# Moving the layer norms' statistics within a round of a shifted-window attention block

## The chip, the cores and the metric

The kernel runs on one core of one Trainium2 chip. The metric is the device time of one execution in microseconds (us); lower is better. A core has five engines that run side by side, each through its own list of instructions in order: TensorE (PE in the profile; its weight loads are shown as PEld), VectorE (DVE), ScalarE (ACT), GpSimd (POOL) and SyncE (SP), which here issues nearly all DMA transfers. Engines wait for each other by semaphores. TensorE writes its products to PSUM, from which VectorE and ScalarE take them into SBUF, the working memory.

## The reference

The input x is (16, 192, 56, 56) in fp32. Layer 0 is a Swin block with windows of 7x7 tokens, shifted by 3, 6 heads of 32; layer 1 a depthwise 3x3 convolution whose filters are computed from the image's mean. All biases are 0 and all gains 1 in the inputs, but the kernel uses them.

```python
h = _ln(jnp.transpose(x, (0, 2, 3, 1)), norm1_g, norm1_b)        # first norm, over 192 channels
h = jnp.roll(h, (-SHIFT, -SHIFT), axis=(1, 2))
win = h.reshape(B, nwh, WS, nww, WS, C).transpose(0, 1, 3, 2, 4, 5).reshape(-1, N, C)
qkv = (win @ qkv_w + qkv_b).reshape(-1, N, 3, HEADS, HD).transpose(2, 0, 3, 1, 4)
q, k, v = (qkv[0] * SCALE, qkv[1], qkv[2])
attn = jnp.einsum('bhqd,bhkd->bhqk', q, k) + bias[None]
attn = jax.nn.softmax(attn + mask, axis=-1)
out = jnp.einsum('bhqk,bhkd->bhqd', attn, v).transpose(0, 2, 1, 3).reshape(-1, N, C)
h = out @ proj_w + proj_b
x1 = x + back_to_the_image(h)
y = _ln(jnp.transpose(x1, (0, 2, 3, 1)), norm2_g, norm2_b)       # second norm
y = jax.nn.gelu(y @ fc1_w + fc1_b, approximate=False) @ fc2_w + fc2_b
x = x1 + jnp.transpose(y, (0, 3, 1, 2))
# layer 1, per image
t = relu(bn(x.mean(axis=(2, 3)) @ w1.T))
wt = (t @ w2.T + b2).reshape(b * DIM, 1, 3, 3) * MASK            # 4 taps of 9 are left
out = depthwise_conv(x, wt) + bias
```

## The kernel before

**Strips and rounds.** An image is cut into 8 bands of 7 rows; a strip is two such bands, one in each half of the 128 partitions, with the 192 channels as 3 groups of 64. An image has NU = 4 strips, the input S = 64. x is kept in SBUF for three images at a time (`xt`, slot b % 3); each strip is normed, attended to and passed through the two layers in place. The main loop at the end runs rounds r = -2 to S + 2 and works in each of them on several strips at different stages: scores and values of strip r, weighted values and projection of strip r - 1, first layer of the MLP for strip r - 2, its second layer for strip r - 3, queries and keys of strip r + 1. When an image's last strip has passed the second layer (the round in which `weighing` is true), its filter taps are computed (`taps`, L958 and L970 to L988); its convolution (`conv`, L1137 and L1152) and the stores of its output (L1035) follow in the three rounds after that.

**The order.** Nothing is issued while the loop runs. Each step is recorded by `add(engine, cost, function, reads, writes, lag)` in a `Plan`. Steps of TensorE keep the order in which they are recorded. For all other engines `Plan.order` plays the list through with the given costs and with `lag` as an extra delay after a transfer, and lets each engine take the step that can start first, then the one whose due time is earliest. So the costs and lags set the order, and a step may be issued far from where it stands in the loop. In the built program every engine's order is fixed.

**PSUM.** Four tiles `ps` are handed out in turn by `bank()`. A product that takes a tile waits until the engine that read the tile's last content, four products before, is done with it.

**A norm's statistics.** `statistics(n, s)` squares the strip's rows on ScalarE (`sq`, L299) and adds the three channel groups of x and of the squares on GpSimd into `fold[:, n]` (L306, L308); n = 0 is the first norm, n = 1 the second. `deviations(norms)` multiplies the folds by a block matrix on TensorE (L322), which gives mean and mean square; then Square on ScalarE (L336), a subtraction on VectorE (L343), and Ln and Exp on ScalarE (L352, L359) make 1/deviation in `rs`. SP sends `rs` to a small DRAM tile (`rsd`, L369) and reads it back twice with a broadcast over 64 partitions into `rb` (L378). `scaled1` (L436, L447) multiplies the first norm's rows by it into `xs1`, read by `queries_keys` (L478) and `values` (L673); `scaled2` (L463) does so for the second norm into `xs2`, read by `first_layer` (L838). The means are folded into the weights. The first rounds (`early`, r < 3) use `full_deviations`, which needs no transfer.

**Attention.** `scores` (L558) writes three tiles; VectorE adds the bias (L584) and takes the maxima (L595), GpSimd subtracts them (L600), ScalarE takes the exponential (L607), VectorE the sums (L612, L613), GpSimd divides (L618). `turn_shares` turns the shares in blocks on VectorE (L629) into `tt`, and ten transfers bring them into `pt` (L635). `values` (L673) are copied by ScalarE (L689), moved by eight transfers into `vb` (L699) and turned on VectorE (L708). `weighted` (L728) multiplies both a round later; its three tiles, j = 0 to 2, are copied in four parts each, i = 0 to 3, into `o1` and `o2` (L755 on ScalarE, L757 on VectorE). `projection` (L799, L785) adds onto x on VectorE (L827). The second layer is L876 with its end on VectorE (L863). The first layer's Gelu (L850) needs another table than Ln and Exp; each change is a table load on ScalarE (L1169).

**TensorE's order in a round before the change:** scores, values, weighted, second layer, projection, queries and keys, first layer, and then the product of `deviations` for the first norm of strip r + 2 and the second norm of strip r - 1. `statistics(0, r + 2)` stand at the start of the round, `load(r + 3)` at its end.

Of the kernel before, what the change touches and what calls it, by code (L numbers as in the profile page):

```python
# [40 lines left out]
def flat(keys):  # L41
    return [x for k in keys for x in (k if isinstance(k, Keys) else (k,))]


class Plan:
# [7 lines left out]
    def add(self, eng, dur, fn, reads=(), writes=(), lag=0.0, slack=60.0, by=None):  # L53
        i = len(self.ops)
        deps = set()
        reads, writes = flat(reads), flat(writes)
        for k in reads:
            if k in self.writer:
                deps.add(self.writer[k])
        for k in writes:  # L60
            if k in self.writer:
                deps.add(self.writer[k])
            deps.update(self.readers.get(k, ()))
        for k in reads:
            self.readers.setdefault(k, []).append(i)
        for k in writes:
            self.writer[k] = i
            self.readers[k] = []
        deps.discard(i)
        self.ops.append((eng, dur, fn, sorted(deps), lag, slack, by))  # L70
# [70 lines left out]
def tile_swin_then_dynamic_conv(  # L141
# [29 lines left out]
    S = B * NU  # L171
# [12 lines left out]
    add = plan.add  # L184
# [21 lines left out]
    rb = sb("rb", 128, 2, UT)  # L206
# [18 lines left out]
    rs = sb("rs", 128, HT)  # L225
# [47 lines left out]
    def load(s, by=None, lag=8.0):  # L273
        b, u = divmod(s, NU)
        t = xt[b % 3]
        xv = x[b].rearrange("(g p) r c -> p g r c", p=64)
        parts = [(0, 0, WS, SHIFT + WS * u)]
        first = SHIFT + LR + WS * u
        if u < NU - 1:
            parts.append((1, 0, WS, first))  # L280
        else:
            parts += [(1, 0, IMG - first, first), (1, IMG - first, WS, 0)]
        for h, lo, hi, at in parts:
            def go(h=h, lo=lo, hi=hi, at=at):
                nc.sync.dma_start(
                    t[P(h), :, 1 + WS * u + lo : 1 + WS * u + hi, :],
                    xv[:, :, at : at + hi - lo, :],
                )
            add("SP", 0.2 * (hi - lo), go, writes=[("x", b % 3, u, h) if lo == 0 else ("x", b % 3, u, 2)], lag=lag, by=by)
# [22 lines left out]
    def deviations(norms):  # L312

        p, pk = bank()
        lanes = slice(64 * norms[0], 64 * norms[-1] + 64)

        def product():
            for k in range(2):
                for n in norms:
                    for h in range(2):  # L320
                        c = 64 * n + 32 * h
                        nc.tensor.matmul(  # L322
                            p[c : c + 32, k, 0:HT],
                            blk,
                            fold[:, n, k, h * HT : (h + 1) * HT],
                            start=True,
                            stop=True,
                            tile_position=(0, c),
                        )

        keys = [("f", n, k) for n in norms for k in range(2)]
        add("PE", 0.33 * len(norms), product, keys + ["blk"], [pk])
        add(
            "ACT",
            0.4,
            lambda: nc.scalar.activation(m2[lanes], p[lanes, 0, 0:HT], AF.Square),  # L336
            [pk],
            ["m2"],
        )
        add(  # L340
            "DVE",
            0.36,
            lambda: nc.vector.tensor_tensor(  # L343
                m2[lanes], p[lanes, 1, 0:HT], m2[lanes], ALU.subtract
            ),
            [pk, "m2"],
            ["m2", "variance"],
        )
        add(
            "ACT",  # L350
            0.45,
            lambda: nc.scalar.activation(m2[lanes], m2[lanes], AF.Ln, bias=eps_t[lanes]),  # L352
            ["m2", "eps", "table"],
            ["m2"],
        )
        add(
            "ACT",
            0.4,
            lambda: nc.scalar.activation(rs[lanes], m2[lanes], AF.Exp, scale=-0.5),  # L359
            ["m2", "table"],  # L360
            ["rs"],
        )
        far[0] += 1
        d = rsd[far[0] % 2]
        dk = ("rsd", far[0] % 2)

        def away():
            lo, hi = 4 * norms[0], 4 * norms[-1] + 4
            nc.sync.dma_start(d[lo:hi], rs[lanes][::16])  # L369

        add("SP", 0.65, away, ["rs"], [dk], lag=4.5)
        dv = d.rearrange("(k a) t -> a k t", a=2)
        ks = slice(2 * norms[0], 2 * norms[-1] + 2)
        for ab in range(2):
            def go(ab=ab):
                src = dv[ab, ks].rearrange("(o k) t -> o k t", o=1)
                dst = rb[P(ab)].rearrange("p n (h t) -> p (n h) t", h=2)
                nc.sync.dma_start(dst[:, ks], src.broadcast_to([64, src.shape[1], HT]))  # L378
            add("SP", 0.65, go, [dk], [("rb", n, ab) for n in norms], lag=4.0)

    def full_deviations():

# [76 lines left out]
    def scaled2(s):  # L459
        xv = rows(s).rearrange("p g r c -> p g (r c)")  # L460
        for g in range(G):
            def go(g=g):
                nc.gpsimd.tensor_tensor(xs2[:, g], xv[:, g], rb[:, 1], ALU.mult)  # L463
            add("POOL", 1.05, go, X(s) + RB(1), [("xs2", g)])
# [246 lines left out]
    def weighted(s):  # L711


        banks = [bank() for _ in range(3)]

        def product(j):
            p = banks[j][0]
            for t in range(4):
                for h in range(2):
                    for w in range(2):  # L720
                        if j < 2:
                            ab, pair, lane = j, t, 64 * h
                            slot, head = 16 * j + h * 8 + pair * 2, 2 * h
                        else:
                            ab, pair, lane = w ^ h, t, 64 * h
                            slot, head = 32 + ab * 8 + pair * 2, 4
                        shares = pt[64 * w : 64 * w + N, :, slot : slot + 2, 0:QL]
                        nc.tensor.matmul(  # L728
                            p[lane : lane + 64, w, t * 128 : t * 128 + 4 * QL],
                            v[64 * w : 64 * w + N, ab, pair, head * HD : (head + 2) * HD],  # L730
                            shares.rearrange("p q k c -> p k q c"),
                            start=True,
                            stop=True,
                            tile_position=(64 * w, lane),
                        )

        for j in range(3):
            p, k = banks[j]
            add(
                "PE",  # L740
                0.7,
                lambda j=j: product(j),
                PTK() + [("v", i) for i in range(2)] + ["ptz"],
                [k],
            )
            for i in range(4):
                lanes = slice(TL * i, TL * i + TL)
                at = (i % 2) * 2 * QL
                src = p[lanes].rearrange("p w (t c) -> p w t c", c=128)[:, :, :, at : at + N]
                if j < 2:  # L750
                    dst = o1[lanes, j].rearrange("p (w t) c -> p w t c", w=2)
                else:
                    dst = o2[lanes]
                if j != 1:
                    add("ACT", 0.5, lambda dst=dst, src=src: nc.scalar.copy(dst, src), [k], [("o", j, i)])  # L755
                else:
                    add("DVE", 0.56, lambda dst=dst, src=src: nc.vector.tensor_copy(dst, src), [k], [("o", j, i)])  # L757
# [859 lines left out]
    def has(s):  # L1617
        return 0 <= s < S

    for r in range(-2, S + 3):  # L1620
# [19 lines left out]
        if r == 0:  # L1640
            load(3)
            load_fc2()
            load_taps()
        if has(r + 2) and r > -2:
            statistics(0, r + 2)
        early = r < 3
        norms = [n for n, s in ((0, r + 2), (1, r - 1)) if has(s) and not early]
        if has(r):
            scores(r)
            if r != 2:  # L1650
# [1 line left out]
                    pass  # L1652
        if r == 2:
            fold_fc1()
        if 2 <= r <= 3:
            deviations([1])
        if has(r - 2):
            scaled2(r - 2)
        if has(r + 1) and r > -2:
            scaled1(r + 1)  # L1660
        if early and r > -2:
# [11 lines left out]
            fold_taps()  # L1673
        if has(r - 1):
            weighted(r - 1)
        if has(r):
            turn_shares()
            turn_values()
# [29 lines left out]
        if has(r - 2):  # L1708
            table("gelu_and_others")
            first_layer(r - 2)  # L1710
            table("natural_log_exp_and_others")
        if norms:
            deviations(norms)
        for b in range(B):
            k = r - (b * NU + NU + 3)
            if b == B - 1 and r == S + 2:
# [10 lines left out]
            elif b < B - 1 and 0 <= k < 3:  # L1727
                conv(b, 2 * k)
                conv(b, 2 * k + 1)
        if has(r + 3) and r >= 1:  # L1730
            load(r + 3)

    with tc.manual_schedule():
        for i in plan.order():
# [75 lines left out]
```

## Time and profile before

| | us |
|---|---|
| median of three runs | 2747.85 (2746.66 to 2749.24) |
| profiled execution, its own time | 2747.47 |
| its span, first to last instruction | 2745.6 |
| TensorE busy | 2703.0 |
| VectorE, ScalarE, GpSimd busy | 1966.0, 1714.7, 1552.0 |
| granted TensorE clock, mean | 0.995 |

The span is what the profiler saw of the core; the execution's own time is 1.9 us longer. A profile's "busy" is the time in which an engine has an instruction running. A line such as `L478 PE MATMUL ps<-xs,wqkv` names the source line, the engine, the operation, and what it writes and reads; brackets at the end tell how long the engine had been idle before and what released it ("issue" where the profile shows no such thing). DMA share is the mean busy share of the core's 16 DMA engines. Over the whole span the DMA engines moved 239.61 MB:

```profile
DMA packets 142563, 239.61 MB, mean 87 GB/s; under 512 B 35148, under 2 KB 100612, under 8 KB 142212
q1 hardware_dynamic: 140360, 232.95, 37.9%
q8 instruction: 258, 4.23, 0.7%
```

The busiest transfers per issue are pt (192 and 96 KB), vb (96 KB), x (294 KB), the outputs (196 KB) and rb (196 KB).

### The profile page before, as it was taken

The page shows a single profiled execution, that of the slowest core. Times are in us where ns is not written, and L with a number is a line of the kernel's source. Part 1 is how long each engine was busy: PE and PEld are TensorE (multiplying, and loading weights), DVE is VectorE, ACT ScalarE, POOL GpSimd, SP SyncE. Part 2 cuts the span into 40 slices and gives each one's busy share as a digit, 9 for nine tenths or more (in the row PEclk, how much of TensorE's full clock was granted, in tenths as well). Part 3 has the DMA queues.
Part 4 walks back from the last instruction along what each step waited for, and adds up shares of the span by engine and source line. Part 5 has one row for each costly group of instructions (what it writes and reads, how often), then busy time and mean ns, then how long its engine had stood idle before and what let it go on. Part 6 is the DMA issues. An engine that isn't in the chain of part 4 may idle for free.

```text
span 2745.6 us, 78133 instructions
## 1 busy us (share of the span) xinstructions
PE 2703.0 (98%) x32871; PEld 1669.1 (61%) x32871; DVE 1966.0 (72%) x3462; ACT 1714.7 (62%) x2787; POOL 1552.0 (57%) x1433
## 2 busy tenths in 40 slices
PE   6999999999999999999999999999999999999998
PEld 4656666666666566566566566566566566666654
DVE  6765776767687676876768777676876767767674
ACT  4556667657567566666666666576666666676553
POOL 6565565565565565565665555555655655655532
PEclk9899999999999999999999999999999999999999
DMA  5623343334425334343343424344253343433231
GB/s 124 127 51 72 83 111 71 86 83 104 92 67 117 69 86 101 72 116 72 78 104 90 106 67 96 73 103 92 67 129 69 75 110 80 113 72 73 60 77 52
DMA packets 142563, 239.61 MB, mean 87 GB/s; under 512 B 35148, under 2 KB 100612, under 8 KB 142212
## 3 DMA queue, kind: packets, MB, share of 16 engines
q1 hardware_dynamic: 140360, 232.95, 37.9%
q8 instruction: 258, 4.23, 0.7%
q10 hardware_dynamic: 1852, 1.66, 0.3%
q14 instruction: 93, 0.76, 0.1%
HBM read 66.81 MB, written 38.98 MB: 39 GB/s over the span
## 4 chain that ended last, share of the span: by engine, by line
PE 96%; DVE 2%; SPq 1%; DMA 0%; issue 0%; ACT 0%; POOL 0%; ACTq 0%; DVEq 0%
PE ps L876 28%; PE ps L838 28%; PE ps L478 14%; PE ps L673 7%; PE ps L558 5%; PE ps L799 5%; PE ps L728 5%; PE ps L785 2%; PE ps L322 2%; DVE sq L972 0%; PE ps L1362 0%; DVE hid L1152 0%; DMA tt<-in_L_conv_qkv_w_dram 0%; PE ps L1342 0%; DVE bt L1522 0%
## 5 line engine op out<-in xcount | busy, mean ns | idle before, releaser
L876 PE MATMUL ps<-hid,wf 128*64 128x392 f32 x4608 | 774.3, 494 | 0.5 <-issue 0.5
L838 PE MATMUL ps<-xs,wf 64*128 64x392 f32 x4608 | 769.5, 489 | 0.0
L838 PEld LDWEIGHTS ps<-xs,wf 64*128 64x128 f32 x4608 | 445.9, 187 | 312.6 <-issue 0.9
L876 PEld LDWEIGHTS ps<-hid,wf 128*64 128x64 f32 x4608 | 330.0, 137 | 408.2 <-issue 369.8
L306 POOL TENSOR_TENSOR fold<-sq 128x392 f32<-128x392 f32 x127 | 129.6, 1021 | 692.9 <-PE ps L322 684.3
L618 POOL TENSOR_TENSOR e<-e,tot 128x784 f32<-128x784 f32 x192 | 321.4, 1685 | 212.2 <-DVE tot L613 208.6
L850 ACT ACTIVATE hid<-ps,b1f 128x784 f32<-128x784 f32 x384 | 342.0, 913 | 137.3 <-PE ps L838 135.0
L478 PE MATMUL ps<-xs,wqkv 64*128 64x392 f32 x2304 | 402.6, 499 | 3.5 <-DVE x L827 1.5
L1152 DVE SCALAR_TENSOR_TENSOR y<-x,wt,y 128x770 f32<-128x770 f32 x270 | 319.1, 1201 | 66.2 <-ACT y L1014 45.3
L478 PEld LDWEIGHTS ps<-xs,wqkv 64*128 64x128 f32 x2304 | 218.6, 188 | 164.9 <-issue 17.0
L600 POOL TENSOR_TENSOR e<-e,top 128x784 f32<-128x784 f32 x192 | 283.3, 1504 | 41.6 <-DVE top L595 41.6
L491 ACT ACTIVATE q<-ps,qbs 128x400 f32<-128x400 f32 (+1 forms) x128 | 68.5, 589 | 319.6 <-PE ps L478 319.6
L612 DVE TENSOR_REDUCE tot<-e 128x16 f32<-128x784 f32 x192 | 182.2, 949 | 107.6 <-ACT e L607 107.6
L755 ACT COPY o<-ps 32x392 f32<-32x392 f32 x512 | 244.3, 477 | 9.5 <-PE ps L728 3.2
L629 DVE STREAM_TRANSPOSE tt<-e 128x512 f32<-128x512 f32 x384 | 245.7, 684 | 1.9 <-POOL e L618 0.4
L766 ACT ACTIVATE x<-x,vecs 128x392 f32<-128x392 f32 x192 | 105.7, 613 | 208.2 <-POOL xs L447 203.5
L343 DVE TENSOR_TENSOR m<-ps,m 128x196 f32<-128x196 f32 (+1 forms) x64 | 23.2, 363 | 273.5 <-ACT m L336 273.5
L673 PE MATMUL ps<-xs,wqkv 64*64 64x196 f32 x4608 | 204.7, 327 | 3.4 <-issue 1.4
L463 POOL TENSOR_TENSOR xs<-x,rb 128x392 f32<-128x392 f32 x192 | 193.5, 1039 | 25.0 <-DMA rb<-rsd 25.0
L306 POOL TENSOR_TENSOR fold<-x 128x392 f32<-128x392 f32 x128 | 132.8, 1038 | 127.7 <-DVE x L827 99.8
L436 POOL TENSOR_TENSOR xs<-x,rb 128x343 f32<-128x343 f32 x191 | 186.0, 1003 | 22.2 <-DMA rb<-rsd 16.8
L584 DVE TENSOR_TENSOR e<-ps,bt 128x784 f32<-128x784 f32 x192 | 175.3, 968 | 12.5 <-ACT hid L850 7.4
(134 smaller groups left out, 3688.1 us busy)
## 6 DMA issues: line engine op xcount, KB each, us to landing
pt<-tt SPq DMA_DIRECT2D x256, 192.0 KB
vb<-kbd SPq DMA_DIRECT2D x488, 96.0 KB
x<-in_x_dram SPq DMA_DIRECT2D x112, 294.0 KB
out_dram<-y SPq DMA_DIRECT2D x135, 196.0 KB
pt<-tt SPq DMA_DIRECT2D x256, 96.0 KB
rb<-rsd SPq DMA_DIRECT2D x118, 196.0 KB
out_dram<-y SPq DMA_DIRECT2D x45, 154.0 KB
x<-in_x_dram SPq DMA_DIRECT2D x16, 168.0 KB
```

Source lines behind the costliest of these rows:

```text
L306: at.tensor_tensor(f, src[:, 0], src[:, 1], ALU.add)
L463: nc.gpsimd.tensor_tensor(xs2[:, g], xv[:, g], rb[:, 1], ALU.mult)
L478: nc.tensor.matmul(p[:, ab, 0:UT], lhs_qk(ab, g, i), d[P(ab), g, 0:UT], start=(g == 0), stop=(g == G - 1), tile_position=(64 * ab, 0),)
L600: nc.gpsimd.tensor_tensor(ev, ev, top[j].broadcast_to([128, 16, N]), ALU.subtract)
L618: nc.gpsimd.tensor_tensor(ev, ev, tot[j].broadcast_to([128, 16, N]), ALU.mult)
L629: nc.vector.transpose(tt[:, kb, 16 * j : 16 * j + 16], src)
L673: nc.tensor.matmul(p[P(wh), ab, 0 : 4 * N], wqkv[P(ab), g, 2 * DIM + 64 * m : 2 * DIM + 64 * m + 64], xs[P(ab), g, wh * 4 * N : (wh + 1) * ...
L755: add("ACT", 0.5, lambda dst=dst, src=src: nc.scalar.copy(dst, src), [k], [("o", j, i)])
L838: nc.tensor.matmul(p[:, ab, 0:UT], wf1[P(ab), g, f * 128 : (f + 1) * 128], xs2[P(ab), g], start=(g == 0), stop=(g == G - 1), tile_position ...
L850: nc.scalar.activation(hid[:, f], p[:, :, 0:UT], AF.Gelu, bias=b1f[:, f : f + 1])
L876: nc.tensor.matmul(p[P(ab), 0, 0:UT], wf2[:, f, g * 64 : (g + 1) * 64], hid[:, f, ab], start=(f == 0), stop=(f == NFC - 1), tile_position= ...
L1152: nc.vector.scalar_tensor_tensor(dst, s_, w[:, g, t : t + 1], dst, ALU.mult, ALU.add)
```

## The change

The product of `deviations` moves in TensorE's order from behind the first layer to between the weighted values and the second layer. In the same place it now serves the first norm of strip r + 2 and the second norm of strip r - 2, and `scaled2(r - 2)` follows it in the same round. `statistics(0, ...)` move from the start of the round to behind the first layer and are for strip r + 3, so that a strip's first norm is made a round earlier against its scaling in `scaled1`. Loads of x are for strip r + 4. The last rounds keep a product for the second norm alone behind the first layer. Of the copies behind `weighted`, ScalarE takes the parts i = 0, 1 of tiles j = 0 and 1 and all of j = 2, and VectorE the parts i = 2, 3 of j = 0 and 1. Both lags of the transfers through DRAM become 5.0 in the plan.

```diff
-        add("SP", 0.65, away, ["rs"], [dk], lag=4.5)
+        add("SP", 0.65, away, ["rs"], [dk], lag=5.0)
...
-            add("SP", 0.65, go, [dk], [("rb", n, ab) for n in norms], lag=4.0)
+            add("SP", 0.65, go, [dk], [("rb", n, ab) for n in norms], lag=5.0)
...
-                if j != 1:
+                if j == 2 or i < 2:
                     add("ACT", 0.5, lambda dst=dst, src=src: nc.scalar.copy(dst, src), [k], [("o", j, i)])
                 else:
                     add("DVE", 0.56, lambda dst=dst, src=src: nc.vector.tensor_copy(dst, src), [k], [("o", j, i)])
...
-        if has(r + 2) and r > -2:
+        early = r < 3
+        if early and r > -2:
             statistics(0, r + 2)
-        early = r < 3
-        norms = [n for n, s in ((0, r + 2), (1, r - 1)) if has(s) and not early]
+        norms = [n for n, s in ((0, r + 2), (1, r - 2)) if has(s) and 3 <= r < S - 1]
         if has(r):
             scores(r)
...
-        if 2 <= r <= 3:
+        if r == 2:
             deviations([1])
-        if has(r - 2):
-            scaled2(r - 2)
+            scaled2(0)
...
         if has(r - 1):
             weighted(r - 1)
+        if norms:
+            deviations(norms)
+        if has(r - 2) and not early:
+            scaled2(r - 2)
         if has(r):
             turn_shares()
             turn_values()
...
             first_layer(r - 2)
             table("natural_log_exp_and_others")
-        if norms:
-            deviations(norms)
+        if has(r + 3) and r > 1:
+            statistics(0, r + 3)
+        if has(r - 1) and r >= S - 2:
+            deviations([1])
...
-        if has(r + 3) and r >= 1:
-            load(r + 3)
+        for s in {0: (), 1: (4, 5)}.get(r, (r + 4,)):
+            if has(s) and r > 0:
+                load(s)
```

## The prediction

> **What bounds the kernel now.** I read first the page's busy times and the chain that ended last, by engine:
>
> ```profile
> PE 2703.0 (98%) x32871; PEld 1669.1 (61%) x32871; DVE 1966.0 (72%) x3462; ACT 1714.7 (62%) x2787; POOL 1552.0 (57%) x1433
> PE 96%; DVE 2%; SPq 1%; DMA 0%; issue 0%; ACT 0%; POOL 0%; ACTq 0%; DVEq 0%
> ```
>
> TensorE (PE) is busy for 2703.0 of 2745.6 us, and the chain is PE's own work: other engines' work counts only where PE is held up. Next I asked for PE's timeline, to see where that is. One round of the steady stage (columns: start, length, engine, line, operation, count):
>
> ```profile
> 214.21 0.87 PE L322 MATMUL ps<-fold,blk 128*32 128x196 f32 x16
> 215.01 2.27 PE L558 MATMUL ps<-kbd,q 64*64 64x98 f32 x96
> 217.10 3.17 PE L673 MATMUL ps<-xs,wqkv 64*64 64x196 f32 x72
> 220.08 2.24 PE L728 MATMUL ps<-pt,v 49*64 49x100 f32 x96
> 222.25 12.07 PE L876 MATMUL ps<-hid,wf 128*64 128x392 f32 x72
> 234.16 2.16 PE L799 MATMUL ps<-o,wp 128*64 128x196 f32 x24
> 236.25 1.23 PE L785 MATMUL ps<-o,wp 64*64 64x196 f32 x24
> 237.40 6.20 PE L478 MATMUL ps<-xs,wqkv 64*128 64x392 f32 x36
> 243.43 12.02 PE L838 MATMUL ps<-xs,wf 64*128 64x392 f32 x72
> ```
>
> Each stage starts where the one before ends, and no line has a bracket for idle time. The next L322 starts at 255.38: 41.17 us for one round. I took the starts of the 58 rounds between the first paired L322 (173.05) and the last (2578.04). About half last 41.16 or 41.17; the sum lies 17.4 us above 58 such rounds. Split by stage and by place in the cycle of four rounds (one image), it is: 4.7 at L799 in the round of an image's filter taps (14 times 0.33: the taps' own matmuls, which stay); 4.6 at L478 in that same round; 6.3 at L673 and L728, in the second round after it; 1.8 scattered. So 12.7 us are stalls, of which 4.9 show as idle and the rest as matmuls drawn out. PE's other idle time lies in the first 131 us (10.75 before the first matmul, 16 more by 115) and behind its last matmul (10.6).
>
> The 6.3 us have a mark. Around the worst of them, PE's timeline shows a gap inside a run of matmuls that all have their inputs, and the view by windows (last columns: granted clock, DMA share, GB/s) shows the DMA engines full just before:
>
> ```profile
> 1007.96 0.99 PE L673 MATMUL ps<-xs,wqkv 64*64 64x196 f32 x17 [0.96 <-issue]
> ```
> ```profile
> 1002.00:1006.00 4.00, 4.00 (x145) 3.56 (x141) 2.97 (x4) 3.28 (x6) 3.21 (x4) 1.00 0.96 242
> ```
>
> Then SP's queue holds ten pt, two x and five out transfers back to back, 1176 + 588 + 784 = 2548 KB by the page's sizes. In the round at 918, with a DMA share of 0.02 to 0.17 at the same stages, there is no gap. The clock is 1.00 throughout.
>
> Last, the timeline of all engines around L322:
>
> ```profile
> 918.43 0.87 PE L322 MATMUL ps<-fold,blk 128*32 128x196 f32 x16
> ...
> 919.39 0.33 ACT L336 ACTIVATE m<-ps 128x196 f32<-128x196 f32 x1
> ...
> 921.92 0.58 SPq L369 DMA_DIRECT2D rsd<-rs  x1
> ...
> 924.54 0.75 ACT L689 ACTIVATE kbd<-ps,bv 128x256 f32<-128x256 f32 x2 [0.25 <-PE ps L673]
> ...
> 927.62 2.30 SPq L378 DMA_DIRECT2D rb<-rsd  x2
> ...
> 933.59 2.91 POOL L436 TENSOR_TENSOR xs<-x,rb 128x343 f32<-128x343 f32 x3 [0.62 <-DMA rb<-rsd]
> ```
>
> From the statistics' product to scaled rows is 15.2 us, mostly two transfers through DRAM. Both scalings follow; PE never waited for them in these rounds.
>
> **The change part by part.** I count from the first score matmul (919.23 = 0). PE then reaches L673 at 2.08, L728 at 5.07, and now L876 at 7.24.
>
> *PE's product.* The number of L322 matmuls is the same: 59 paired groups and five single ones before and after (one single group moves from round 3 to round 62). One group takes 0.80 (start to next start), 0.78 as a single one between L673 and L728. Behind L728 and ahead of L876 it has not stood; the nearest rows (0.78, 0.80, and L876's own 11.90 or 12.00 by its neighbours) differ by 0.1, so 59 x ±0.1 = ±6 us at most, and I take 0, the value of the identical group.
>
> *The o copies.* Eight on ScalarE, four on VectorE as before, so no work is added; the first two tiles' halves swap. This matters because the second layer's first PSUM bank was last used by the values; with the extra bank taken just ahead, it becomes that of the first weighted product. That product ends at about 5.8; ScalarE is free at 6.06 (L689 ends 925.29) and copies twice 0.48, to 7.0. VectorE adds the bias and takes three maxima, 0.9 + 2.74 + 2.71 = 6.35, then copies twice 0.57, to 7.5. L876 now starts at 7.24 + 0.80 = 8.04. It is covered by 0.5 us; four copies on ScalarE would have ended at 8.0. Cost 0, uncovered 59 x what they are late.
>
> *The second norm's chain.* The product starts at 7.24 and L838 needs the scaled rows at 28.42 + 0.80 = 29.22 (243.43 - 215.01, plus the inserted group). The table load (1.28 at 919.74) leaves the chain, four o2 copies of 0.48 enter it: Square 8.2 to 8.53, copies to 10.4, Ln 0.46 and Exp 0.37, so rs at 11.3. In SP's queue the rsd and the two rb transfers now stand behind all eight vb transfers: 6.06 + 8 x 0.62 = 11.0, just covered. Then as in the lines above, 5.7 to the rb issue and 6.0 to landing, 23.0; scaled2's three multiplies, 3.0: 26.0. The changed kernel's order on GpSimd puts the three shares L618 and two fold additions ahead; they end at about 20.7. Spare: 3.2 us. The slowest of the 58 rounds took 13.5 from rsd to landing, which would leave 1.4. Behind a late rb wait, on GpSimd, scaled2 and then the next folds, whose product follows 10 us after they would be ready; on SP, pt. Cost 0.
>
> *The first norm and its loads.* Its chain is a whole round ahead: in the changed order scaled1 runs between the first and second of GpSimd's subtractions L600 and ends some 13 us ahead of L478. Statistics for it and the x loads (two or three transfers of 294 KB or less each) issue as often as before, a round earlier; the x loads still wait for the convolution to free their rows. Cost 0, covered by 41 us of round; no gain either, as PE did not wait there (but for 0.7 at 45 us, which stays).
>
> *What does get better.* GpSimd no longer holds two of three shares behind scaled1, which waits for rb (933.59). All six turns of the shares now stand ahead of or beside the projection, so pt leaves at about +23, not at +33.8 (953.01). The burst at the second round after the taps loses its 1176 KB and keeps 1372. The third round's burst (six out, four x, 1960 KB) comes some 4 us earlier in the round and also loses its pt; it had two gaps, 1.6 us together, in 15 rounds. Bounds: all 6.3 us go, or as many come back at the third round. I take two thirds, -4: the row nearest to the new bursts is that third round, nearly free of gaps.
>
> *The taps' round.* L478's second bank waits for the projection's first additions on VectorE, which stand behind the taps' products (L972, 1.98 beside a GpSimd multiply, 0.76 alone); all shift by 0.80 together. 0, between -4.6 and +4.
>
> Sum: 2745.6 - 4 = 2741.6 of span; the profiled run took 1.9 more than its span (2747.47), so 2743.5. That run is 0.4 under the median of 2747.85; I predict 2743.5.
>
> The Trainium skill ("Runtime: NRT & Kernel Launch", section "Instruction fetch mechanics") says that an engine streams its instructions in 16 KiB blocks by a DMA queue of its own and that crossing a block is mostly hidden; it speaks against my one gain. The page's instruction queue (258 packets, 4.23 MB) agrees with the block size, but the gaps beside a DMA share of 0.96 suggest that a full set of engines uncovers it. By the rule alone the sum would be 2747.5.
>
> **The rivals.** About 0.2%, 5.5 us, is what a measurement of this kernel can tell from no change.
>
> 1. *Every steady stall goes*: also the taps' wait, if scaled2 no longer runs beside L972. For it: L972's 1.98 against 0.76. Against: scaled2 would run just then. 2747.85 - 12.7 + 2 of scatter = 2737. Chance 0.20.
> 2. *The stalls only move*: what the bursts lose is made up at the third round, where x and out are issued closer. 2747.85 less 0 = 2748. Chance 0.10.
> 3. *The norm's chain ends last*: rb lands after 26 and L838 waits for scaled2. For it: 1.4 us left in the slowest round, and in the third round three x loads (2.0 us of issue; 588 KB, 2.5 us at the 235 GB/s seen at 1002 to 1008) now stand between rsd and rb: 29.22 - 1.4 + 2.5 is 1.1 late. In one round of four 15 x 1.1 = 16.5: 2764; in all 59, 65: 2813. It decides once rb lands 3.2 us later than at 918. Against: SP waits 5.7 for rsd anyway. Chance 0.13, at 2764.
> 4. *The second layer waits for its bank*: if VectorE's copies are 1 us later than 7.5, 0.5 x 59 = 30: 2777; decided by 0.5 us. Chance 0.07.
>
> **How the numbers follow.** My forecast has 0.50, with 2738 to 2749 as its own range (stalls all gone or none, and a part of the ±6); about a quarter of it falls under 2742.3. Faster: 0.20 + 0.13 = 0.33. Slower: 0.13 + 0.07 = 0.20. The rest, 0.47, is no change. The range runs from 2736 to 2757, leaving out a tenth below and the worse half of rivals 3 and 4 above.
>
> **What would show it.** L728 directly followed by L322 and L876 without a bracket, rounds of 41.17; scaled rows L463 done some 3 us ahead of L838; pt issued about 11 us earlier; no gap at L673 or L728 in the second round after the taps. A bracket at L838 from L463 is rival 3, one at L876 from L755 or L757 rival 4. I'd be wrong outright if the x loads, a round earlier, held back vb or rsd in SP's queue.

## The result and the profile after

| | us | against before, 95% interval |
|---|---|---|
| before, median of six runs | 2747.33 (2745.74 to 2749.24) | |
| changed, median of six runs | 2766.43 (2762.47 to 2771.37) | 1.007 (1.0057 to 1.0083) |
| profiled execution of the changed kernel, its span | 2771.37, 2769.6 | |

The change costs 19 us, 0.7%. The prediction, 2743.5 with a range of 2736 to 2757, was wrong. The profiled execution of the changed kernel is the slowest of its six, 4.9 us above their median, so sums taken from its profile come out somewhat larger than 19. Busy times and chain on the page of the changed kernel:

```profile
PE 2707.7 (98%) x32871; PEld 1731.9 (63%) x32871; DVE 1967.6 (71%) x3462; ACT 1691.6 (61%) x2787; POOL 1559.0 (56%) x1433
PE 83%; ACT 7%; DVE 7%; issue 3%; DMA 1%; POOL 0%; SPq 0%; ACTq 0%; DVEq 0%; POOLq 0%
```

TensorE is busy for about as long as before, but the chain of work that ended last now runs 14% of the time through ScalarE and VectorE (2% before). TensorE is held up by them, in two places, for about 29 us together; shorter stalls elsewhere give back some 7. TensorE's waits name the two places (waiting line, releaser: us in total, times, longest):

```profile
PE ps L673 <- DVE e L584: 10.9, 15, 0.9
PE ps L876 <- DVE o L757: 9.9, 54, 0.2
```

Only one wait of 0.9 us at L673 on L584 was there before, and none at L876 on L757. TensorE's timeline of one round shows the second:

```profile
1181.61 2.26 PE L558 MATMUL ps<-kbd,q 64*64 64x98 f32 x96
1183.69 3.16 PE L673 MATMUL ps<-xs,wqkv 64*64 64x196 f32 x72
1186.68 2.24 PE L728 MATMUL ps<-pt,v 49*64 49x100 f32 x96
1188.85 0.87 PE L322 MATMUL ps<-fold,blk 128*32 128x196 f32 x16
1189.90 12.07 PE L876 MATMUL ps<-hid,wf 128*64 128x392 f32 x72 [0.18 <-DVE o L757]
1201.78 2.19 PE L799 MATMUL ps<-o,wp 128*64 128x196 f32 x24
1203.90 1.23 PE L785 MATMUL ps<-o,wp 64*64 64x196 f32 x24
1205.05 6.20 PE L478 MATMUL ps<-xs,wqkv 64*128 64x392 f32 x36
```

I call the time from the start of one group of products to the start of the next the group's stage. The L322 stage, up to L876, takes 1.05 us instead of 0.80. L558 of the next round starts at 1223.03, so the round takes 41.42 us instead of 41.16. The timeline of all engines at that place shows what L876 waits for:

```profile
1187.61 1.95 ACT L755 COPY o<-ps 32x392 f32<-32x392 f32 x4
...
1188.61 2.33 DVE L757 COPY o<-ps 32x392 f32<-32x392 f32 x4 [0.66 <-ACT o L755]
...
1188.85 0.87 PE L322 MATMUL ps<-fold,blk 128*32 128x196 f32 x16
```

VectorE has its third maximum done at 1187.95 and then stands idle for 0.66 us until ScalarE has made its two copies of the first weighted tile. Only then does it make its own two, of 0.58 us each; they end at about 1189.8, and L876, which writes into that bank, starts at 1189.90.

The other place is the round that follows the taps' round. First the kernel before, then the changed one, both from the timeline of all engines (L985 and L988 finish an image's filter taps, L1137 and L1152 are the convolution with them, L584 adds the bias to the scores):

```profile
1112.72 0.74 DVE L985 TENSOR_REDUCE wt<-sq 128x12 f32<-128x576 f32 x1
...
1113.96 2.10 DVE L502 TENSOR_SCALAR kbd<-ps,bq,mask 128x784 f32<-128x784 f32 x2
...
1114.59 1.03 ACT L1137 ACTIVATE y<-x,vecs,wt 128x784 f32<-128x784 f32 x1
1115.72 12.02 PE L838 MATMUL ps<-xs,wf 64*128 64x392 f32 x72
...
1128.47 2.27 PE L558 MATMUL ps<-kbd,q 64*64 64x98 f32 x96
1129.44 2.74 DVE L584 TENSOR_TENSOR e<-ps,bt 128x784 f32<-128x784 f32 x3
```
```profile
1129.68 0.69 DVE L534 TENSOR_SCALAR kbd<-ps,bq,mask 64x392 f32<-64x392 f32 x1 [0.75 <-ACT kbd L525]
1130.40 0.75 DVE L985 TENSOR_REDUCE wt<-sq 128x12 f32<-128x576 f32 x1
...
1135.38 1.04 ACT L1137 ACTIVATE y<-x,vecs,wt 128x784 f32<-128x784 f32 x1
1136.46 5.70 DVE L1152 SCALAR_TENSOR_TENSOR y<-x,wt,y 128x770 f32<-128x770 f32 x4 [4.21 <-ACT y L1137]
...
1139.25 2.27 PE L558 MATMUL ps<-kbd,q 64*64 64x98 f32 x96
...
1142.19 2.74 DVE L584 TENSOR_TENSOR e<-ps,bt 128x784 f32<-128x784 f32 x3
...
1143.22 2.22 PE L673 MATMUL ps<-xs,wqkv 64*64 64x196 f32 x48 [0.71 <-DVE e L584]
```

Before, L985 runs 15.75 us ahead of the score products L558, and L584 follows their start by 0.97. In the changed kernel L985 runs 8.85 us ahead of them, because it now stands behind the steps L629, L502 and L534 on VectorE. ScalarE adds to it: L1137 starts 4.02 us after the taps are done (L988, at 1131.36) and not 0.75, for it now stands behind steps of the first layer and the norm (L515, L850, L299). So the convolution's first four L1152, 1.43 us each, reach into the scores; L584 follows 2.94 us after the products' start, and the second part of L673 waits for the bank that L584 reads. The L673 stage takes 3.93 us instead of 2.99.

I took the starts of L838 on TensorE in 60 steady rounds of every profile and sorted the rounds by their place in an image's cycle of four. In this table each number is the sum over 15 rounds of what they take above 41.16 us. The first of the 15 rounds called "next" lies at the start and follows no taps' round. The other rows are experiments of the next section.

| kernel | taps' round | next | second after | third after | sum |
|---|---|---|---|---|---|
| before | 9.8 | 0.3 | 6.6 | 1.7 | 18.4 |
| changed | 9.0 | 17.8 | 4.9 | 8.0 | 39.8 |
| copies by tile | 5.4 | 13.9 | 0.7 | 4.1 | 24.1 |
| taps' end first | 8.9 | 3.5 | 4.0 | 6.1 | 22.6 |
| both mended | 5.1 | 1.0 | 0.4 | 3.7 | 10.1 |
| norms before weighted | 7.6 | 2.8 | 2.4 | 3.2 | 16.1 |
| same, copies by tile | 7.5 | 2.5 | 2.5 | 3.0 | 15.5 |
| before, copies shared | 23.3 | 0.6 | 4.2 | 1.7 | 29.8 |
| before, loads ahead | 9.7 | 0.4 | 5.8 | 1.7 | 17.6 |
| before, shares first | 5.1 | 3.9 | 0.1 | 2.9 | 11.9 |
| before, shares first from the fifth round | 5.1 | 0.6 | 0.1 | 4.1 | 9.9 |
| both mended, shares first | 14.5 | 11.0 | 23.2 | 21.4 | 70.0 |

The changed kernel's 21.4 us more are 60 times 0.26 at L322 (15.6) and 14 times 0.94 at L673 (13.2; the fifteenth wait in the list lies at the start and was there before), together 28.8, less 7.4 of gains elsewhere.

### The profile page after: what moved, and what is told of

Read it like the earlier page. It is cut to its first block, busy times and chain, and to the rows that moved or that the text cites. A ratio compares the mean times of both kernels' runs of the same rounds, so it can differ in the third digit from the quotient of the medians.

```text
span 2769.6 us, 78471 instructions
## 1 busy us (share of the span) xinstructions
PE 2707.7 (98%) x32871; PEld 1731.9 (63%) x32871; DVE 1967.6 (71%) x3462; ACT 1691.6 (61%) x2787; POOL 1559.0 (56%) x1433
## 4 chain that ended last, share of the span: by engine, by line
PE 83%; ACT 7%; DVE 7%; issue 3%; DMA 1%; POOL 0%; SPq 0%; ACTq 0%; DVEq 0%; POOLq 0%
PE ps L876 28%; PE ps L838 21%; PE ps L478 14%; PE ps L673 6%; PE ps L799 5%; PE ps L558 4%; DVE y L1152 3%; PE ps L785 3%; ACT o L755 2%; DVE o L757 1%; ACT hid L850 1%; DVE kbd L534 1%; ACT q L515 1%; ACT kbd L689 1%; ACT kbd L525 1%
## 5 line engine op out<-in xcount | busy, mean ns | idle before, releaser
L876 PE MATMUL ps<-hid,wf 128*64 128x392 f32 x4608 | 774.1, 493 | 11.0 <-DVE o L757 9.9
L838 PE MATMUL ps<-xs,wf 64*128 64x392 f32 x4608 | 770.0, 489 | 1.1 <-POOL xs L463 1.0
L838 PEld LDWEIGHTS ps<-xs,wf 64*128 64x128 f32 x4608 | 445.7, 187 | 314.4 <-POOL xs L463 3.3
L876 PEld LDWEIGHTS ps<-hid,wf 128*64 128x64 f32 x4608 | 380.5, 137 | 383.2 <-issue 350.6
L600 POOL TENSOR_TENSOR e<-e,top 128x784 f32<-128x784 f32 x192 | 295.4, 1557 | 328.4 <-DVE top L595 328.4
L850 ACT ACTIVATE hid<-ps,b1f 128x784 f32<-128x784 f32 x384 | 342.2, 914 | 113.4 <-PE ps L838 111.1
L1152 DVE SCALAR_TENSOR_TENSOR y<-x,wt,y 128x770 f32<-128x770 f32 x270 | 339.0, 1283 | 91.5 <-ACT y L1137 59.2
L478 PE MATMUL ps<-xs,wqkv 64*128 64x392 f32 x2304 | 401.4, 499 | 1.7 <-DVE e L584 1.2
L306 POOL TENSOR_TENSOR fold<-sq 128x392 f32<-128x392 f32 x127 | 138.4, 1090 | 449.3 <-ACT sq L299 446.2
L618 POOL TENSOR_TENSOR e<-e,tot 128x784 f32<-128x784 f32 x192 | 285.5, 1504 | 125.5 <-DVE tot L613 99.4
L584 DVE TENSOR_TENSOR e<-ps,bt 128x784 f32<-128x784 f32 x192 | 175.3, 968 | 221.9 <-ACT hid L850 177.5
L478 PEld LDWEIGHTS ps<-xs,wqkv 64*128 64x128 f32 x2304 | 220.6, 189 | 160.1 <-issue 16.9
L863 DVE SCALAR_TENSOR_TENSOR x<-ps,vecs,x 128x392 f32<-128x392 f32 x192 | 118.6, 618 | 174.2 <-PE ps L876 128.3
L629 DVE STREAM_TRANSPOSE tt<-e 128x512 f32<-128x512 f32 x384 | 241.6, 677 | 0.3 <-POOL fold L306 0.2
L306 POOL TENSOR_TENSOR fold<-x 128x392 f32<-128x392 f32 x128 | 142.5, 1114 | 160.1 <-PE ps L478 80.2
L673 PE MATMUL ps<-xs,wqkv 64*64 64x196 f32 x4608 | 207.7, 328 | 11.9 <-DVE e L584 10.9
L502 DVE TENSOR_SCALAR kbd<-ps,bq,mask 128x784 f32<-128x784 f32 x128 | 134.1, 1090 | 108.9 <-PE ps L478 108.9
L463 POOL TENSOR_TENSOR xs<-x,rb 128x392 f32<-128x392 f32 x192 | 190.9, 1024 | 24.7 <-DMA rb<-rsd 24.7
L689 ACT ACTIVATE kbd<-ps,bv 128x256 f32<-128x256 f32 x366 | 137.1, 425 | 95.8 <-PE ps L673 95.8
```

The source lines that it names most:

```text
L306: at.tensor_tensor(f, src[:, 0], src[:, 1], ALU.add)
L478: nc.tensor.matmul(p[:, ab, 0:UT], lhs_qk(ab, g, i), d[P(ab), g, 0:UT], start=(g == 0), stop=(g == G - 1), tile_position=(64 * ab, 0),)
L600: nc.gpsimd.tensor_tensor(ev, ev, top[j].broadcast_to([128, 16, N]), ALU.subtract)
L618: nc.gpsimd.tensor_tensor(ev, ev, tot[j].broadcast_to([128, 16, N]), ALU.mult)
L629: nc.vector.transpose(tt[:, kb, 16 * j : 16 * j + 16], src)
L673: nc.tensor.matmul(p[P(wh), ab, 0 : 4 * N], wqkv[P(ab), g, 2 * DIM + 64 * m : 2 * DIM + 64 * m + 64], xs[P(ab), g, wh * 4 * N : (wh + 1) * ...
```

## The experiments

Each was run in five rounds beside the kernel before. Ratios are to the kernel before, with 95% intervals; its medians were 2746.75 us in the first four, 2747.62 in the next four and 2748.35 in the last two. The changed kernel was not run again beside them; differences to it are taken to its median of 2766.43, which stood beside 2747.33, so they are uncertain by up to 1 us.

### Copies by tile again

```diff
-                if j == 2 or i < 2:
+                if j != 1:
```

> The changed kernel with one part undone: the four copies of the first tile of weighted values are all ScalarE's again and the four of the second all VectorE's, as in the kernel before. Theory: in the changed kernel VectorE's two copies of the first tile wait for ScalarE's two (0.66 us in its timeline), so the bank that the second layer takes next comes free 0.25 us late in each of some 60 rounds. With ScalarE alone on that tile its four copies also run one after another, but VectorE no longer holds them up; the time from a round's first L322 product to its first L876 product should come from 1.06 back to 0.80 to 0.85 us, and the time by 11 to 15 us, to about 2753. Rival: the statistics that now follow the copies take the bank late however the copies are split; the 1.06 stays and so does 2766. A second rival: four copies of 0.58 us in a row on ScalarE end later than two and two, and L876 waits longer than 0.25: above 2770.

Measured 2752.93 us, 1.0022 (1.0012 to 1.0033): 13.5 less than the changed kernel. The L322 stage is back at 0.80 in all four kinds of round, and no wait of L876 on the copies is left; the wait of L673 on L584 stays (10.8 us, 15 times). The steady rounds take 15.7 us less. The theory holds, and both rivals fall.

### The end of the taps first

```diff
-        add("DVE", 0.9, fin, ["sq", "b2t"], [("wt", b % 2)])
+        add("DVE", 0.9, fin, ["sq", "b2t"], [("wt", b % 2)], slack=12.0)
```

> The changed kernel with the last step of the taps (L985 and L988 on VectorE) put ahead of the product rows and norm steps that stand before it there, right behind L827. Theory: the taps come 7 us late in the changed kernel, so the first convolution's four L1152 on VectorE run into the next round's scores and L584 behind them frees the bank of the second values product late; that is the 3.93 instead of 2.99 us of the L673 stage in every fourth round, 15 times. With the taps early that stage should be back at 3.0 and the time 14 us lower, about 2752. Rival: the convolution is late because of its own place or of the norm's steps, not of the taps: L673 stays at 3.9 and the time at 2766. The L322 stage stays at 1.06 by both.

Measured 2752.02 us, 1.0024 (1.0015 to 1.0033): 14.4 less than the changed kernel. The L673 stage after the taps' round is at 2.99, and the L322 stage at 1.05 in three rounds of four and at 1.00 in the round after the taps' round. The theory holds, and the rival falls.

### Both

The two edits together.

> Both edits at once in the changed kernel: the copies split by tile and the taps' end right behind L827, with the norm's deviations still behind the weighted values. Theory: the two losses lie in different rounds and stages and add: 11 to 15 and 14 us, to 2737 to 2741, with the L322 stage at 0.80 to 0.85 and the L673 stage after the taps' round at 3.0. Rival: the two share a cause (VectorE's load in all), so that one mended does most of it: the sum of both is then no more than some 16 us, about 2750.

Measured 2738.13 us, 0.9973 (0.9963 to 0.9982), faster than both kernels: 28.3 less than the changed kernel, where the single edits took 13.5 and 14.4. They add, so the losses are separate, and without them the change costs nothing. The page:

```profile
PE 2698.6 (99%) x32871; PEld 1663.0 (61%) x32871; DVE 1926.1 (70%) x3462; ACT 1697.5 (62%) x2787; POOL 1523.3 (56%) x1433
PE 96%; DVE 2%; DMA 1%; SPq 0%; ACT 0%; POOL 0%; issue 0%; ACTq 0%; DVEq 0%; POOLq 0%
```

The chain is TensorE's own work again, and the steady rounds lie 10.1 us above 60 times 41.16, of which the taps' own matmuls are 5.1.

### The norm's product ahead of the weighted values

```diff
+        if norms:
+            deviations(norms)
         if has(r - 1):
             weighted(r - 1)
-        if norms:
-            deviations(norms)
         if has(r - 2) and not early:
             scaled2(r - 2)
```

> The changed kernel with the norm's deviations placed ahead of the weighted values and not behind them; scaled2, the first norm's lead and the earlier loads stay. The first bank of the second layer then follows the deviations' own tile in the ring of banks and not the first tile of weighted values; the order that results also has the taps' end right behind L827. Theory: both losses go, L322 stage at 0.80 and L673 after the taps' round at 3.0, while the gain of the second round after the taps (no wait at L673 and L728, 6.3 us) and of the taps' round (4.6 us) stays: 2737 to 2741, faster than the kernel before. Rival: the lost time belongs to the first norm's lead and the loads, and comes back in another place: 2750 to 2766.

Measured 2745.94 us, 0.9995 (0.9985 to 1.0005): 20 less than the changed kernel, but no better than the kernel before; the forecast was missed by 5 to 9 us. The two losses did go (L322 stage 0.80, L673 after the taps' round like in any other round). A new one came, in TensorE's timeline:

```profile
506.75 3.17 PE L673 MATMUL ps<-xs,wqkv 64*64 64x196 f32 x72
509.85 0.87 PE L322 MATMUL ps<-fold,blk 128*32 128x196 f32 x16
510.65 2.29 PE L728 MATMUL ps<-pt,v 49*64 49x100 f32 x96
512.87 12.07 PE L876 MATMUL ps<-hid,wf 128*64 128x392 f32 x72
```

Nothing waits, and no stage has a bracket, but L673 takes 3.10 us to the next start and L728 2.22, where with L322 behind both it is 2.99 and 2.17. That is 0.16 in each of 60 rounds, 9.6 us: the whole miss. The kernel before has one such round, at 133.82, in which a single L322 stands between the two: there too L673 takes 3.10 and L728 2.22. The next run asked whether it is the order on TensorE or the sharing of the copies.

### The same, with the copies by tile

> The changed kernel with the deviations ahead of the weighted values, as in the run that came to 2745.9, and with the copies split by tile as well. In that run L322 stands between L673 and L728 on TensorE; its L673 stage is 3.09 instead of 2.99 and its L728 stage 2.22 instead of 2.17, in every round. Theory: that 0.15 to 0.16 us in each of some 60 rounds (9 us) is the price of L322's place among the products of values, so it stays: 2744 to 2748, with the same two stages. Rival: the copies shared between two engines cost it; with the copies by tile the stages go back and the time is 2736 to 2740.

Measured 2745.82 us, 0.9991 (0.9983 to 1.0); the stages are 3.09 and 2.22 as with shared copies. So the price belongs to L322's place on TensorE. What in that place costs it was not tried. One candidate is the shape of the products' tiles, which the timeline shows behind the operands: 64\*64 and 49\*64 for L673 and L728, 128\*32 for the L322 between them. In this order sharing the copies costs nothing: with shared copies VectorE sits idle for ScalarE's 198 times, 110.3 us in all, with copies by tile never, and TensorE takes the same time.

### The kernel before with shared copies

```diff
-                if j != 1:
+                if j == 2 or i < 2:
```

> The kernel before with the changed kernel's sharing of the copies and nothing else. Theory: sharing a tile makes VectorE wait for ScalarE here too, but the bank that the second layer takes first was last read by other work in this kernel, so no stage of TensorE moves: L322 stage 0.80, time 2745 to 2750. Rival: the wait holds up VectorE's later work, the first layer's or the second norm's, wherever the banks lie: 10 to 15 us more, about 2760.

Measured 2760.18 us, 1.0045 (1.0032 to 1.0058): the time is the rival's, and my theory holds for the bank alone. The L322 stage is 0.80, as it said. The loss sits in the taps' round, where the L478 stage takes 7.24 us instead of 6.34. Timelines of the kernel before, then of this one:

```profile
1106.97 2.97 POOL L618 TENSOR_TENSOR e<-e,tot 128x784 f32<-128x784 f32 x2
1107.74 0.50 PE L958 MATMUL ps<-w1t,pooled 128*64 128x48 f32 x12
...
1110.05 0.76 DVE L972 SCALAR_TENSOR_TENSOR sq<-trow,w2r 128x576 f32<-128x576 f32 x1
```
```profile
1112.09 0.50 PE L958 MATMUL ps<-w1t,pooled 128*64 128x48 f32 x12
1112.42 2.97 POOL L618 TENSOR_TENSOR e<-e,tot 128x784 f32<-128x784 f32 x2
...
1114.03 1.97 DVE L972 SCALAR_TENSOR_TENSOR sq<-trow,w2r 128x576 f32<-128x576 f32 x1
1115.93 2.08 DVE L827 TENSOR_TENSOR x<-ps,x 128x196 f32<-128x196 f32 x12
...
1116.87 4.22 PE L478 MATMUL ps<-xs,wqkv 64*128 64x392 f32 x24 [0.94 <-DVE x L827]
```

In the kernel before, L972 starts 0.11 us after GpSimd's two L618 have ended. With shared copies these end 3.30 us after L958's start and not 2.20, so L972 runs beside them and takes 1.97 instead of 0.76; L827 and with it L478 come late. The timeline a little earlier shows why GpSimd is 1.1 us later:

```profile
1099.78 2.44 ACT L755 COPY o<-ps 32x392 f32<-32x392 f32 x5 [0.73 <-DVE o L757]
...
1100.29 0.57 DVE L757 COPY o<-ps 32x392 f32<-32x392 f32 x1 [0.54 <-ACT o L755]
...
1100.89 0.97 DVE L595 TENSOR_REDUCE top<-e 128x16 f32<-128x784 f32 x1
...
1102.25 2.35 ACT L607 ACTIVATE e<-e 128x784 f32<-128x784 f32 x3
```

The two engines wait for each other in turn, and ScalarE's eight copies take 5.25 us in all (from 1096.97) where the kernel before makes them in 3.91. So the exponentials L607 and the first L618 start 1.36 us later, counted from L958. Sharing thus costs time here away from the bank; that this delay is the whole cause was read from the timelines and not tried.

### The kernel before with the rows loaded a round ahead

```diff
-        if has(r + 3) and r >= 1:
-            load(r + 3)
+        for s in {0: (), 1: (4, 5)}.get(r, (r + 4,)):
+            if has(s) and r > 0:
+                load(s)
```

> The kernel before with the rows loaded a round ahead and nothing else. Theory: these loads are far from any user in both kernels and cost or bring nothing: 2745 to 2750. Rival one: they are what stood beside the late moves of the shares, so that the gaps at L673 and L728 go or move with them: 2740 to 2743. Rival two: they hold back the moves of values or shares on SP's queue: above 2752.

Measured 2744.84 us, 0.9992 (0.9983 to 1.0001). The second round after the taps' round keeps 5.8 us of gaps (6.6 before). The loads neither cost nor bring what is looked for, and did not make the gaps there.

### The kernel before with the shares first

```diff
-            add("POOL", 1.9, share, [("tot", j)], [("e", j)])
+            add("POOL", 1.9, share, [("tot", j)], [("e", j)], slack=0.0)
```

> The kernel before with GpSimd's three L618 (shares) put ahead of L436 of the next round, so that the transposes L629 and the moves of the shares out of tt go earlier in the round; nothing of the norms or loads is moved. Theory: the kernel before loses 6.3 us to gaps without a releaser in the L673 and L728 stages of the second round after the taps, because there the moves of the shares start 11 us late beside the other transfers; with the moves early these gaps go: 2740 to 2743. Rival: the gaps come from the norm's round trip through DRAM or from the loads, which this does not move: 2746 to 2749. Should GpSimd's L436 of the next round come late by this order, L478 waits: above 2750.

Measured 2769.96 us, 1.0083 (1.0071 to 1.0095): a miss by its total, but the place decides. The steady rounds take 6.5 us less than before, and the second round after the taps' round lies at 0.1 instead of 6.6. The first L838 starts at 148.5 us instead of 119.7. TensorE's waits show that start:

```profile
PE ps L478 <- POOL xs L447: 17.0, 2, 9.9
...
PE ps L1342 <- DVE x L827: 8.8, 1, 8.8
```

There the shares stand in front of the scaled rows that L478 waits for: the third forecast, in the first rounds alone. So the next run left the first rounds as they were.

```diff
+            add(..., **({"slack": 0.0} if s > 3 else {}))
```

> The kernel before with GpSimd's L618 (shares) first from the fifth round on; the first rounds keep their order. With shares first in all rounds the 60 steady rounds together were 6.5 us shorter than before (11.9 instead of 18.4 us above 60 times 41.16) but the first rounds 29 us longer. Theory: the steady gain is real and the loss is the start's alone: 2739 to 2743, with the taps' round back from 41.81 to 41.50 and the second round after it from 41.60 to 41.2. Rival: the steady rounds ran well only because of their longer start, and the gaps come back: 2746 to 2749.

Measured 2742.42 us, 0.9972 (0.996 to 0.9983), as the theory said. The ten pt transfers are issued 17.3 to 18.5 us after the round's first score product, where the kernel before issues them at 32.9 to 34.2 in three rounds of four and at 25.3 to 26.3 in the third after the taps' round. Wherever they are early, the gaps in the second round after the taps' round are gone: 0.1 here, 0.4 with both edits (pt at 22.1 to 22.9); with the loads moved and pt still at 32.9 to 34.0, they stay.

### Both edits and the shares first

The edit of the run before this one, in the kernel with both edits.

> Both edits in the changed kernel (copies by tile, the taps' end behind L827; 2738.1) and the shares first from the fifth round on. What is left there above 60 times 41.16 is 10.1 us: 5.1 for the taps' own matmuls and 5.0 in scattered gaps without a releaser. Theory: the shares are early in that kernel already, so this changes nothing: 2737 to 2740. Rival one: the scattered gaps follow the moves of the shares and shrink: 2733 to 2736. Rival two: GpSimd's L436 comes late and L478 waits: above 2742.

Measured 2800.58 us, 1.0186 (1.0173 to 1.0199). The theory and the first rival failed; the time is above the second rival's 2742, but not for its reason, as all of L478's waits for L447 come to 2.0 us. The largest wait of TensorE is L876 on ScalarE's copies, 40.7 us in 49 waits. The timeline of one round:

```profile
1198.84 1.43 ACT L755 COPY o<-ps 32x392 f32<-32x392 f32 x3
...
1200.29 0.86 ACT L607 ACTIVATE e<-e 128x784 f32<-128x784 f32 x1
...
1201.17 0.48 ACT L755 COPY o<-ps 32x392 f32<-32x392 f32 x1
...
1201.70 12.07 PE L876 MATMUL ps<-hid,wf 128*64 128x392 f32 x72 [0.82 <-ACT o L755]
```

With an earlier share the plan puts an exponential, L607, between the third and the fourth copy of the first weighted tile. Again it is that tile's bank and L876. With the deviations behind the weighted values there is little room at this bank: one step of 0.86 us among the copies is enough for a wait of 0.82.

## Why the prediction was wrong

*The step that failed: the o copies.* It put ScalarE's two copies at 6.06 to 7.0 and VectorE's at 6.35 to 7.5, side by side, ahead of L876 at 8.04: "covered by 0.5 us". Counted from the same zero (1181.61) the round above has ScalarE's from 6.00, VectorE free at 6.34 and L322 at 7.24, all as forecast. But VectorE's copies start at 7.00, when ScalarE's are done, and L876 at 8.29. The two engines take turns on one PSUM tile; I counted them as independent. With a tile for each engine they copy side by side, as in the kernel with both edits:

```profile
1874.38 1.94 ACT L755 COPY o<-ps 32x392 f32<-32x392 f32 x4
...
1875.13 2.29 DVE L757 COPY o<-ps 32x392 f32<-32x392 f32 x4 [0.42 <-PE ps L728]
```

VectorE starts there as soon as its product is done, though both engines write into the same `o1`; so it is the PSUM tile and not the target on which they take turns. The price is 0.25 to 0.26 in each of some 60 rounds, 13.5 us by the run that undoes it. This is rival 4 (chance 0.07): the second layer waits for its bank behind VectorE's copies, 0.65 us later than 7.5, at half the price that I gave it. Why they would be late, it did not say.

The Trainium skill ("PSUM — Partial Sum Buffer", section "PSUM bank collisions raise a hardware error") says that two engines may not access one bank in the same 32-partition quadrant at once, two reads included, that different quadrants of a bank may be read at once, and that guarding a whole bank is the simple version. Here ScalarE reads partitions 0 to 63 and VectorE 64 to 127, and the trace shows VectorE idle for 0.66 us with ScalarE's copy as the releaser: in this program the wait goes by the tile. Whether the chip would let both read was not tried.

*A term that was missing: the end of the taps.* The step on the taps' round said that "all shift by 0.80 together". I read the changed order around L827 and L972 and not what follows on VectorE, where L985 and L988 had gone behind L629, L502 and L534. That made the convolution late, and L673 waited for L584 in 14 rounds, 0.94 us each; it cost 14.4 us by the run that undoes it. No rival held it. What in the change moved the two steps was not taken apart; with the deviations ahead of the weighted values they are back behind L827.

*The taps' round.* Forecast 0, between -4.6 and +4. L478 went from 6.34 to 6.03, 15 times 0.31: the whole 4.6. L827 starts 2.49 to 2.51 us after L958 in 14 of the 15 rounds, instead of 2.71 to 3.20. In the rounds shown above L971 takes 0.98 us and not 1.48, beside GpSimd's L463 and not its L618. L463 ends 0.1 us ahead of L972. So the taps' wait went, as rival 1 had it, and not as I held against it, that scaled2 "would run just then". Nor was it L972 alone that took long in the kernel before: it took 1.98 in 5 of the 15 rounds, and in the other ten L971 was drawn out to 1.20 to 1.60.

*The bursts.* Forecast -4: pt leaves at +23, the gaps of the second round go and a part comes back in the third. Measured pt at 22.3 to 23.7; without the 3.9 us that L322's 0.26 makes in 15 rounds, the second and third rounds after the taps' round together went from 8.3 to 5.1, -3.2 (-4.2 with both edits). Right in mechanism and size: 5.6 us went in the second round and 2.4 came back in the third, so rival 2 has less than half of it. The order of the shares alone does the same in the kernel before, and the loads do not. That the fetch of instructions opened the gaps, as the prediction suspected, no run shows.

*TensorE's product* costs 0 behind L728, as taken: stage 0.80 where nothing is late, and rounds of 41.16. The ±6 was too narrow for other places, as 9.6 us for L322 between L673 and L728 shows. The prediction's own row for that place, the round at 133.82, held it: L322 alone was read there, at 0.78, and not its neighbours.

*The second norm's chain and the first norm's loads.* Forecast 0 with 3.2 us to spare. In the round above the scaled rows L463 are done at 1205.5 and L838 starts at 1211.08: 5.5 to spare and not 3.2. Rival 3 did not come, nor the harm by loads that would have made me "wrong outright".

So the sum by the measured terms is -4.6 - 3.2 + 15.6 + 13.2 = +21.0, against 21.4 in the steady rounds and 19.1 by the medians. With its two losses mended, the change gives -8.6 us; the order of the shares alone gives the kernel before -5.9. The scattered gaps without a releaser, some 5 us over 60 rounds in each of these two kernels, stay unexplained.

## What to carry to other kernels

When a product is inserted between others, ask which bank each later product inherits, and follow that bank's last reader to its end; two engines on one tile are to be counted one after the other unless a trace shows them together, and their turns can delay other work too, as in the kernel before with shared copies. When a planner sets the order, compare each engine's whole order over a full cycle, not only around the moved step: half the loss here came from two small steps that the change does not mention. A move that loses may still hold a gain, and mending one loss at a time tells which part to keep.

## What the runs showed of the hardware

- The place of a group of 16 matmuls that itself takes 0.80 us wherever it stands changes its neighbours: between L673 and L728 these take 0.16 us more together (3.10 and 2.22) than with the group behind both (2.99 and 2.17), without any wait.
- VectorE's L972 took 0.76 us alone and 1.97 beside GpSimd's L618; L1152 took 1.43 us each in the changed kernel's group of four and 1.03 in the kernel before. With the copies shared in the kernel before, GpSimd's L618 ended 1.1 us later and L478 took 0.9 us more in every taps' round.
